# A Mamba, attention and mixture-of-experts layer pair on one core: wide state scans with the carried state in the tile, convolution made ahead, last attention in two halves

## The chip, the core and the metric

The kernel runs on one core of a Trainium2 chip. The core has TensorE (PE) for matrix products, VectorE (DVE), ScalarE (ACT) and GpSimd (POOL) for elementwise work, and SyncE (SP), which here only issues DMAs; 16 DMA engines move data between DRAM and the on-chip memory (SBUF), and matrix products land in a small accumulator memory (PSUM). The metric is the device time of one launch in microseconds, the median of several runs. All data are 32-bit floats.

## What is computed

The input is 8 images of 256 channels and 32 x 32 pixels, taken as 8 sequences of 1024 tokens with 256 features. Layer 0 is a Mamba block with a feed-forward block behind it, layer 1 attention with a mixture of experts behind it. Cut to what matters here:

```python
# layer 0, per image: x is [1024 tokens, 256]
xm, z = split(layernorm(x) @ W_in)                       # 512 features each
xm = silu(sum(shift(xm, k) * conv_w[:, k] for k in range(4)) + conv_b)
dt, Bm, Cm = split(xm @ W_x)                             # 16, 16 and 16 features
dt = softplus(dt @ W_dt + b_dt)
for t in tokens:                                         # 512 features x 16 states
    h = exp(dt[t] * A) * h + dt[t] * xm[t] * Bm[t]
    y[t] = sum_over_states(h * Cm[t])
x = x + ((y + xm * D) * silu(z)) @ W_out
x = x + gelu(layernorm(x) @ W1 + b1) @ W2 + b2
# layer 1
q, k, v = heads(layernorm(x))                            # 8 heads of 32
t = x + concat(softmax(q k' / sqrt(32) + column_bias) v) @ Wo + bo
u = layernorm(t)
w = softmax(mean_over_tokens(u) @ Wr + br)               # one routing per image, top 2 of 8 experts
out = t + layernorm(u + sum(w[e] * expert(e, u) for e in top2))
```

The recurrence over `t` is the heart of it: 512 x 16 independent first-order recurrences of 1024 tokens for each of 8 images.

## The kernel before

**Tiling.** Features lie on the 128 partitions, tokens along the free dimension. Each image is cut into two chunks of 512 tokens, so there are 16 chunks, 0 to 15; an even chunk is the first half of an image, an odd one the second. The 512 inner features are four groups of 128, handled as two halves of two groups. A chunk has 32 *steps*: 16 states times two halves. One step works on a tile of 128 partitions x 2 rows x 512 tokens (1024 elements).

**A step** (g = 0 to 511). `decay` (line 891) lets ScalarE make exp(dt * A) for both rows into `da_all`, which has two places, used in turn. `inputs` (908) lets VectorE multiply xm * dt by the row B of that state into a slot `hb` of the pool h4. `scan` (920) runs the recurrence in place on VectorE with the scan instruction. In an even chunk the state starts at zero, and one scan of 1024 elements covers both rows: `decay` keeps the first decay factor of the second row at zero, which restarts the recurrence there. In an odd chunk the state comes from the even one, each row has its own, and there are two scans of 512 elements with the tile `state` as their start value. After an even step, GpSimd copies the last column into `state`. `sums` (943) lets VectorE multiply by the row C, and GpSimd issues a DMA that adds the tile onto the accumulator `dx` of that half; the slot is free again when this DMA has landed. There are four such slots, and a fifth (the memory of the weight `w_z`) once all gates are made.

**Streams around the steps.** Everything else is written as Python generators ("streams"), and a small model of the queues' times (line 62) decides at build time where in each engine's instruction order their parts are put: after each part of a step `advance` (2129) emits what the model has as ready, more urgent kinds first (`URGENT`). The engines then run these orders as they were written, each in its own order; nothing is reordered on the chip. The streams are:

- `park` (958): for chunks 2 to 15, far ahead, layer norm, both halves of W_in, and storing the convolution's input (`xin_d`) and silu(z) (`sz_d`) in DRAM.
- `prologue(i)` (685): for chunks 2 to 15 it calls `conv_parked` (635), which loads the convolution's input with its shifts from DRAM, convolves it and applies Silu; then dt by softplus, whose terms GpSimd adds with accumulating DMAs, and the rows B and C. It starts at step FRONT[i-1] of the chunk before. CONV[i] chooses the convolution: four multiply-accumulate passes, the first on ScalarE and three on VectorE (0), or products with diagonal weights `taps` on TensorE (1). SOFT[i] chooses between two forms of softplus: 1 saves a VectorE operation for one more accumulating DMA.
- `gate_part` (991) loads silu(z) at step GATE[i]; `epilogue` (1039) follows after the chunk's last step: gating, W_out, layer norm, the feed-forward block.
- `attention` (1540): image by image, when the epilogues of both its chunks are done. It works through 32 units (two head groups x two query chunks x eight key blocks): scores on TensorE, Exp on ScalarE, products with v on TensorE; the denominators are products on TensorE too, but for the last image they are sums on VectorE (`dsum`).
- `route` (1717) and the experts: small VectorE operations choose two experts, GpSimd gathers their weights with six indirect DMAs per expert, and the products run on TensorE.

Where TensorE would sit idle, filler products ("warm") are put in, so that its clock stays up. Line 98 of the profile is the helper through which all compute instructions go, line 95 that of the DMAs.

Of the kernel before, what the change touches and what calls it, by code (L numbers as in the profile page):

```python
# [17 lines left out]
P = 128  # L18
B, C, L = 8, 256, 1024
KC = C // P  # L20
CH = 512
# [33 lines left out]
def hybrid_kernel(ctx: ExitStack, tc: tile.TileContext, a: dict, out: bass.AP):  # L55
# [46 lines left out]
    def vec_cost(op, out, *ins):  # L102
        n, into = width(out), str(out)
        chained = op == "scalar_tensor_tensor" and vec.into == into
        vec.into = into
        if op == "tensor_tensor_scan":
            return (0.125 if n == CH else 0.07) + n * 2.08e-3
        return (0.2 if n < P else 0.065) + n * 1.04e-3 + 0.2 * chained
# [42 lines left out]
    w_z = load("w_z", [P, KC, DI], a["W_in"].rearrange("(k p) n -> p k n", p=P)[:, :, DI:])  # L151
# [28 lines left out]
    mean_c = const.tile([P, 1], F32, name="mean_c")  # L180
    pool.memset(mean_c, 1.0 / C)
    mean_w = mean_c.to_broadcast([P, P])
    zero_c = const.tile([P, 1], F32, name="zero_c")
    pool.memset(zero_c, 0.0)
    zero_w = zero_c.to_broadcast([P, P])
    pick = const.tile([P, 4], F32, name="pick")
# [3 lines left out]
    wm_out = const.tile([P, ND], F32, name="wm_out")  # L190
    wm_2 = const.tile([P, HID // P], F32, name="wm_2")
    wm_o = const.tile([P, KC], F32, name="wm_o")
    mean_b = const.tile([P, 1], F32, name="mean_b")
    pick3 = const.tile([P, 4], F32, name="pick3")
    eps_t = const.tile([P, 1], F32, name="eps_t")
# [9 lines left out]
    bq4 = const.tile([P, NG], F32, name="bq4")  # L205
    bk4 = const.tile([P, NG], F32, name="bk4")
# [7 lines left out]
    bq4s = const.tile([P, NG], F32, name="bq4s")  # L214
    ok = const.tile([P, 1], F32, name="ok")
    qs = const.tile([P, 1], F32, name="qs")


    conv_tail = const.tile([P, NCH, ND, KW - 1], F32, name="conv_tail")

# [15 lines left out]
    bad = const.tile([P, 1], F32, name="bad")  # L236
    loads_e = const.tile([P, E], F32, name="loads_e")
    rev_e = const.tile([P, E], F32, name="rev_e")
    base1 = const.tile([P, KC], F32, name="base1")
    base2 = const.tile([P, NF], F32, name="base2")  # L240

    xin_d, t_d, xf_d, x1_d, xc_d, mu_d, mus_d = {}, {}, {}, {}, {}, {}, {}
# [29 lines left out]
    FRONT = (7, 13, 4, 4, 1, 14, 10, 1, 13, 1, 10, 6, 1, 5, 10)  # L272
    GATE = (20, 4, 30, 30, 22, 7, 30, 18, 28, 25, 5, 28, 30, 30, 12, 26)
    CONV = (0, 0, 0, 1, 1, 0, 0, 0, 0, 0, 0, 0, 0, 1, 0, 0)
    SOFT = (1, 0, 0, 1, 0, 0, 0, 0, 1, 0, 1, 0, 0, 0, 0, 0)

    POLL, PARK = -1.0, 2

# [37 lines left out]
    class Owner:  # L318


        def __init__(self, slots, peak, gives=0, held=0):
            self.slots, self.peak, self.gives, self.held = slots, peak, gives, held
            slots.owners.append(self)

        def take(self, name):
            while not (self.slots.ready() and self.slots.safe(self)):
                yield POLL
            self.held += 1
            return self.slots.now(name)
# [66 lines left out]
    def layernorm(  # L396
# [9 lines left out]
        if kept is not None:  # L406
# [10 lines left out]
            if kept < PARK:  # L417
                row = work_pool.tile([P, KW - 1 + CH], F32, name=f"row_{name}", tag="xp", bufs=2)
                row = row[:, :P]
# [13 lines left out]
            yield model.end if kept < PARK else max(landed, model.end)  # L433
            kept_at = sp.dma_start(xc_d[kept], dst)
# [120 lines left out]
    def conv_dve(i, xn, mem):  # L555
# [4 lines left out]
        for d in range(ND + 2):  # L560
            if d > 2 and d % 2:
                for t in range(1, KW):
                    for n in (d - 3, d - 2):
                        y = xm[n // 2][:, n % 2, :]
                        vec.scalar_tensor_tensor(
                            y, xps[n][:, t : t + CH], V("conv_w", n * KW + t), y,
                            ALU.mult, ALU.add,
                        )
            if 0 < d <= ND:
                h, q = divmod(d - 1, 2)  # L570
                xp = work_pool.tile([P, KW - 1 + CH], F32, name=f"xp_{i}_{d}", tag="xp", bufs=2)
                xps.append(xp)
                act.copy(xp[:, : KW - 1], conv_tail[:, c, d - 1, :])
                act.activation(xp[:, KW - 1 :], ps, AF.Identity, bias=b_in[:, d - 1 : d])
                banks.put(ps)
                if c < NCH - 1:
                    act.copy(conv_tail[:, c + 1, d - 1, :], xp[:, CH:])
# [16 lines left out]
    def conv_pe(i, xn, mem):  # L594
# [3 lines left out]
        while not set_up:  # L598
            yield POLL
        xm, xp, ps, ps2 = [], None, None, None  # L600
        for d in range(ND + 1):
            if d < ND:
                if d % 2 == 0:
                    xm.append((yield from mem.take(f"xm_{i}_{d // 2}")))

                ps2 = yield from banks.take(f"xin_{i}_{d}")
                for k in range(KC):
                    pe.matmul(
                        ps2, w_in[:, k, d * P : (d + 1) * P], xn[:, k, :],
                        start=(k == 0), stop=(k == KC - 1),  # L610
                    )
            if d:
                for t in range(KW):
                    for r in range(4):
                        rows = slice(HD * r, HD * r + HD)
                        pe.matmul(
                            ps[rows, :], taps[rows, (d - 1) * KW + t, :], xp[rows, t : t + CH],
                            start=(t == 0), stop=(t == KW - 1),
                        )
                if c < NCH - 1:  # L620
                    act.copy(conv_tail[:, c + 1, d - 1, :], xp[:, CH:])
            yield
            if d:
                h, q = divmod(d - 1, 2)
                act.activation(xm[h][:, q, :], ps, AF.Identity, bias=V("conv_b", d - 1))
                banks.put(ps)
            if d < ND:
                xp = work_pool.tile([P, KW - 1 + CH], F32, name=f"xp_{i}_{d}", tag="xp", bufs=2)
                act.activation(xp[:, KW - 1 :], ps2, AF.Identity, bias=b_in[:, d : d + 1])
                act.copy(xp[:, : KW - 1], conv_tail[:, c, d, :])  # L630
                ps = ps2
            yield
        return xm

    def conv_parked(i, mem):


        b, c = divmod(i, NCH)
        skip = 0 if c else KW - 1
        xm = []  # L640
        for h in range(NHALF):
            xps = []
            xm.append((yield from mem.take(f"xm_{i}_{h}")))
            for q in range(2):
                xp = work_pool.tile([P, KW - 1 + CH], F32, name=f"xp_{i}_{h}_{q}", tag="xp", bufs=2)
                landed = sp.dma_start(
                    xp[:, skip:], xin_d[b][h, :, q, c * CH - (KW - 1) + skip : (c + 1) * CH]
                )
                if skip:
                    act.copy(xp[:, :skip], conv_tail[:, 0, 0, :])  # L650
                xps.append(xp)
            yield landed
            if CONV[i]:
                for q in range(2):
                    d = 2 * h + q
                    ps = yield from banks.take(f"cv_{i}_{d}")
                    for t in range(KW):
                        for r in range(4):
                            rows = slice(HD * r, HD * r + HD)
                            pe.matmul(  # L660
                                ps[rows, :], taps[rows, d * KW + t, :], xps[q][rows, t : t + CH],
                                start=(t == 0), stop=(t == KW - 1),
                            )
                    yield
                    act.activation(xm[h][:, q, :], ps, AF.Identity, bias=V("conv_b", d))
                    banks.put(ps)
                continue
            for q in range(2):
                d = 2 * h + q
                act.activation(  # L670
                    xm[h][:, q, :], xps[q][:, :CH], AF.Identity, bias=V("conv_b", d),
# [3 lines left out]
            for t in range(1, KW):  # L675
                for q in range(2):
                    y = xm[h][:, q, :]
# [1867 lines left out]
```

## Time and profile before

| | us |
|---|---|
| median of three runs (3398.92 to 3409.55) | 3402.78 |
| the profiled execution | 3395.24 |
| its span, first to last instruction | 3393.4 |
| VectorE busy | 2993.7 |
| TensorE busy, fillers of the tile "warm" included | 3141.3 |
| fillers of the tile "warm" | 366.0 |
| ScalarE busy | 2467.8 |
| GpSimd busy | 1104.5 |
| HBM, mean over the span | 107 GB/s |

The profile is one execution on the chip. Its page gives each engine's busy time, the span cut in 40 slices with the busy share of each in tenths, the DMA queues, the chain that ended last, and groups of equal instructions: engine, operation, output tile <- input tiles, shape, count, then busy time and mean length of one in ns, then the idle time of the engine before them and what ended it. The trace behind it can be asked for stages, single instructions in order of time, and waits ("engine tile line <- what it waited for: total us, times, longest"). Buffer numbers are left out of the tiles' names, and a slot in the memory of `w_z` appears under that name.

### The profile page before, as it was taken

The numbers are of one execution on the slowest core, as the hardware profiler recorded it, in microseconds if no ns is written. First come the engines' busy times: TensorE is split into PE (matmuls) and PEld (weight loads), VectorE is DVE, ScalarE is ACT, GpSimd is POOL, SyncE is SP. The second block draws the span as 40 slices with busy tenths as digits, with TensorE's granted clock in tenths as the row PEclk, the third lists the DMA queues.
The fourth block names the chain that finished last, engine by engine and source line by source line (L and its number), as shares of the span: only waits on it lengthen the run. The fifth ranks groups of instructions, "written<-read, shape, count | busy, mean of one in ns | idle before, by whom it ended". The sixth has DMA issues, their size and how long they took to land. (4 is left out here: it accounts for less than half of the span.)

```text
span 3393.4 us, 44585 instructions
## 1 busy us (share of the span) xinstructions
PE 3141.3 (93%) x16359; PEld 1387.0 (41%) x16359; DVE 2993.7 (88%) x3140; ACT 2467.8 (73%) x3610; POOL 1104.5 (33%) x1072
## 2 busy tenths in 40 slices
PE   8888988999899999999999899999899989999998
PEld 5444443433343334333444344333443343334343
DVE  6999999899999979899999999999999999962561
ACT  4766756678867887687779777787768868864643
POOL 0242145313432235334353245133542453211010
PEclk9989989999999999999999999999999989999999
DMA  4877899989988898889998999799998998972140
GB/s 138 237 204 189 218 219 219 227 209 232 222 218 228 195 214 202 211 206 217 225 250 190 224 228 216 185 217 219 232 237 201 227 224 186 211 171 71 39 96 23
DMA packets 216134, 668.21 MB, mean 197 GB/s; under 512 B 31200, under 2 KB 42592, under 8 KB 215904
## 3 DMA queue, kind: packets, MB, share of 16 engines
q0 software_dynamic: 106112, 373.88, 56.5%
q1 hardware_dynamic: 109792, 291.38, 25.3%
q8 instruction: 130, 2.13, 0.2%
q14 instruction: 100, 0.82, 0.1%
HBM read 269.20 MB, written 92.93 MB: 107 GB/s over the span
## 5 line engine op out<-in xcount | busy, mean ns | idle before, releaser
L98 ACT ACTIVATE da_all<-dt,vecs 128x512 f32<-128x512 f32 (+1 forms) x1024 | 699.4, 717 | 287.9 <-DVE hb L98 244.8
L95 POOL DMA_DIRECT2D dx<-hb x449 | 397.3, 890 | 1363.5 <-DVE hb L98 960.8
L98 DVE TENSOR_TENSOR hb<-xm,bc 128x1024 f32<-128x1024 f32 x449 | 540.0, 1203 | 22.5 <-issue 19.8
L98 DVE TENSOR_TENSOR_SCAN hb<-da_all,state,hb 128x512 f32<-128x512 f32 x448 | 552.7, 1268 | 4.2 <-ACT da_all L98 4.1
L98 ACT ACTIVATE pt<-sc 128x1024 f32<-128x1024 f32 x512 | 494.6, 1018 | 81.5 <-PE sc L98 70.9
L98 DVE TENSOR_TENSOR hb<-hb,bc 128x1022 f32<-128x1022 f32 (+1 forms) x449 | 546.7, 1218 | 0.0
L98 DVE TENSOR_TENSOR_SCAN hb<-da_all,hb 128x1024 f32<-128x1024 f32 x225 | 514.2, 2285 | 8.3 <-ACT da_all L98 8.3
L98 PE MATMUL warm<-mean_c,zero_c 128*128 128x256 f32 x1182 | 366.0, 433 | 48.9 <-ACT z L98 11.5
L98 POOL COPY state<-hb 128x2 f32<-128x2 f32 x225 | 330.6, 1471 | 206.4 <-DVE hb L98 201.2
L98 PE MATMUL sc<-qk,qk 32*128 32x512 f32 x2048 | 337.7, 647 | 18.2 <-ACT pt L98 17.1
L98 PEld LDWEIGHTS warm<-mean_c,zero_c 128*128 128x128 f32 x1182 | 219.6, 206 | 191.7 <-PE warm L98 73.3
L98 PE MATMUL num<-pt,v 128*32 128x512 f32 x2048 | 279.6, 616 | 13.2 <-DVE ot L98 13.2
L98 PE MATMUL den<-pt,ecb 128*32 128x512 f32 x1792 | 239.0, 604 | 0.0
L98 PE MATMUL re<-he,g 128*128 128x512 f32 x472 | 221.6, 615 | 18.5 <-ACT sz L98 7.8
L98 PE MATMUL facc<-fh,w 128*128 128x512 f32 x512 | 232.8, 601 | 5.9 <-ACT fo L98 2.4
L98 PE MATMUL fh<-x_f,w 128*128 128x512 f32 x480 | 227.1, 604 | 7.2 <-DVE x_f L98 2.5
L98 PE MATMUL he<-xe,g 128*128 128x512 f32 x448 | 219.0, 615 | 5.7 <-issue 3.5
L98 ACT ACT_TABLE_LOAD x159 | 204.0, 1283 | 3.5 <-PEq L2532 0.7
L98 PEld LDWEIGHTS sc<-qk,qk 32*128 32x128 f32 x2048 | 101.0, 185 | 198.3 <-ACT pt L98 80.3
L98 PEld LDWEIGHTS facc<-fh,w 128*128 128x128 f32 x512 | 95.4, 192 | 132.3 <-issue 118.1
L98 PEld LDWEIGHTS re<-he,g 128*128 128x128 f32 x472 | 89.9, 196 | 133.2 <-issue 103.8
L98 PEld LDWEIGHTS fh<-x_f,w 128*128 128x128 f32 x480 | 86.5, 190 | 133.9 <-issue 100.3
(422 smaller groups left out, 4705.4 us busy)
## 6 DMA issues: line engine op xcount, KB each, us to landing
dx<-hb POOLq DMA_DIRECT2D x449, 512.0 KB, 7.8
bc<-bc_d SPq DMA_DIRECT2D x256, 512.0 KB
dx<-w_z POOLq DMA_DIRECT2D x63, 512.0 KB, 6.7
dt<-e POOLq DMA_DIRECT2D x36, 512.0 KB, 9.5
dt<-u POOLq DMA_DIRECT2D x30, 512.0 KB, 11.4
xin_d<-z SPq DMA_DIRECT2D x28, 512.0 KB
sz_d<-z SPq DMA_DIRECT2D x28, 512.0 KB
sz<-sz_d SPq DMA_DIRECT2D x28, 512.0 KB
```

Source lines behind the costliest of these rows:

```text
L95: f(*args, **kw)
L98: return f(*args, **kw)
```

## The change

**Two-row slots and wide scans.** The tiles of h4 and `da_all` get one more column per row, 2 x 513. Column 0 of each row of `da_all` is set to zero once. Column 0 of each row of `hb` holds the start value: zero in even chunks (set by GpSimd where the slot isn't clean), in odd chunks a copy of `state` that GpSimd makes in `inputs`. One scan of 1026 elements then serves both kinds of chunk. The accumulator `dx` becomes 2 x 513 as well, and the accumulating DMA moves 1025 elements from the second column on.

```diff
     def inputs(g):
+        if i % NCH:
+            pool.at = max(pool.at, vec.at)
+            pool.tensor_copy(hb[:, :, 0], state[:, s, 2 * h : 2 * h + 2])
+            das[g, 2] = pool.at + 0.3
+            clean.discard(id(hb))
+        elif id(hb) not in clean:
+            pool.at = max(pool.at, vec.at)
+            pool.memset(hb[:, :, 0], 0.0)
+            das[g, 2] = pool.at + 0.3
+            clean.add(id(hb))
-        vec.tensor_tensor(hb, xd, bc[:, 0, :].unsqueeze(1).to_broadcast([P, 2, CH]), ALU.mult)
+        vec.tensor_tensor(
+            hb[:, :, 1:], xd, bc[:, 0, :].unsqueeze(1).to_broadcast([P, 2, CH]), ALU.mult
+        )
-    def scan(g, q):
+    def scan(g):
...
-        if c == 0:
-            if q:
-                both = hb.rearrange("p a t -> p (a t)")
-                vec.tensor_tensor_scan(
-                    both, da_all[:, g % 2].rearrange("p a t -> p (a t)"), both, 0.0,
-                    ALU.mult, ALU.add,
-                )
-        else:
-            vec.tensor_tensor_scan(
-                hb[:, q, :], da_all[:, g % 2, q, :], hb[:, q, :], state[:, s, d : d + 1],
-                ALU.mult, ALU.add,
-            )
+        for q in range(3):
+            vec.at = max(vec.at, das.pop((g, q), 0.0))
+        vec.tensor_tensor_scan(
+            flat(hb), flat(da_all[:, g % 2]), flat(hb), 0.0, ALU.mult, ALU.add
+        )
     def sums(g):
-        me["landed", h] = pool.dma_start(out=me["acc", h], in_=hb, accum_op=ALU.add)
+        me["landed", h] = pool.dma_start(
+            out=me["acc", h][:, 1:], in_=flat(hb)[:, 1:], accum_op=ALU.add
+        )
```

In the loop over steps the two decays of step g+2 now both follow the one scan of step g.

**Convolution and Silu ahead.** `park` now convolves and applies Silu for chunks 2 to 15 and stores the result (`xm_d`) in place of the convolution's input; `prologue` loads it. `conv` replaces `conv_pe` and `conv_parked`. The tables change; in CONV, chunks 2 to 6, 8 and 9 are on TensorE (3, 4 and 13 before), in SOFT chunk 1 alone (3, 8 and 10 before; entry 0 is used by neither).

```diff
     def prologue(i: int):
-        mem = Owner(t4, 8, 6)
+        mem = Owner(t4, 9, 6)
         if i < PARK:
...
         else:
-            xm = yield from conv_parked(i, mem)
-        for t in xm:
-            act.activation(t, t, AF.Silu)
-        lnexp()
+            xm = []
+            for h in range(NHALF):
+                xm.append((yield from mem.take(f"xm_{i}_{h}")))
+                landed = sp.dma_start(xm[h], xm_d[i][h])
+            yield landed
     def park():
-            xi = yield from gates(i, mem, xn, 0)
+            xm = yield from (conv if i else conv_first)(i, xn, mem)
+            for t in xm:
+                act.activation(t, t, AF.Silu)
+            lnexp()
             yield
             for h in range(NHALF):
-                mem.put(xi[h], at=sp.dma_start(xin_d[b][h, :, :, c * CH : (c + 1) * CH], xi[h]))
+                mem.put(xm[h], at=sp.dma_start(xm_d[i][h], xm[h]))
-    FRONT = (7, 13, 4, 4, 1, 14, 10, 1, 13, 1, 10, 6, 1, 5, 10)
-    GATE = (20, 4, 30, 30, 22, 7, 30, 18, 28, 25, 5, 28, 30, 30, 12, 26)
-    CONV = (0, 0, 0, 1, 1, 0, 0, 0, 0, 0, 0, 0, 0, 1, 0, 0)
-    SOFT = (1, 0, 0, 1, 0, 0, 0, 0, 1, 0, 1, 0, 0, 0, 0, 0)
+    FRONT = (4, 13, 2, 8, 2, 7, 11, 18, 14, 8, 1, 4, 7, 5, 19)
+    GATE = (27, 7, 13, 30, 30, 18, 29, 15, 23, 21, 6, 26, 27, 30, 24, 27)
+    CONV = (1, 0, 1, 1, 1, 1, 1, 0, 1, 1, 0, 0, 0, 0, 0, 0)
+    SOFT = (1, 1, 0, 0, 0, 0, 0, 0, 0, 0, 0, 0, 0, 0, 0, 0)
```

The start of the diagonal weights `taps` is moved ahead of the other one-time work, the model's VectorE costs are refined, and a rule (`spare`) keeps some of the 25 large SBUF slots free for the prologue before `park`, the experts and the attention take theirs.

**Last attention in halves.** `attention_last` handles the eighth image. It starts when the epilogue of chunk 14 is done and the attention before it has ended, makes q, k and v of that chunk, and runs the 8 units whose queries and keys both lie in it; after the epilogue of chunk 15 it does the other 24. Both head groups keep a sum open in PSUM.

```diff
+        yield from operands(0)
...
+        yield from run_units([(g, 0, j) for g in range(NG) for j in range(NT // 2)])
+        while ("e", b * NCH + 1) not in done:
+            yield POLL
...
+        yield from operands(1)
+        yield from run_units(
+            [(g, 0, j) for g in range(NG) for j in range(NT // 2, NT)]
+            + [(g, 1, j) for g in range(NG) for j in range(NT)]
+        )
```

**Joined routing.** In `route` the row numbers for both weight matrices, and both bias vectors of an expert, are made by one operation each where there were two: seven small VectorE operations per image for fourteen.

## The prediction

> **What bounds the kernel now.** I read the page first, then busy time by stage, then VectorE's waits, then the order of single instructions.
>
> ```profile
> span 3393.4 us, 44585 instructions
> PE 3141.3 (93%) x16359; PEld 1387.0 (41%) x16359; DVE 2993.7 (88%) x3140; ACT 2467.8 (73%) x3610; POOL 1104.5 (33%) x1072
> DVE  6999999899999979899999999999999999962561
> DMA  4877899989988898889998999799998998972140
> ```
>
> VectorE (DVE) is full until slice 35 and nearly idle after it: a scan stage, then a tail. The last scan step ends at 3014 us. By stage (us, then busy time of PE, PEld, DVE, ACT, POOL, then granted clock, DMA share, GB/s):
>
> ```profile
> 64.00:3014.00 2950.00, 2737.99 (x14374) 1194.65 (x14375) 2815.40 (x2793) 2252.69 (x3320) 1064.42 (x1017) 0.96 0.90 215
> 3014.00:3093.00 79.00, 76.15 (x460) 36.23 (x455) 20.83 (x61) 34.93 (x54) 14.10 (x15) 1.00 0.46 111
> 3093.00:3126.00 33.00, 33.00 (x100) 17.52 (x99) 2.45 (x2) 13.94 (x18) 2.31 (x3) 1.00 0.19 63
> 3126.00:3270.00 144.00, 142.83 (x800) 51.97 (x800) 93.58 (x149) 99.91 (x116) 9.15 (x9) 1.00 0.28 59
> 3270.00:3394.00 124.00, 103.02 (x382) 54.74 (x377) 25.68 (x73) 35.07 (x52) 12.85 (x13) 0.95 0.13 40
> ```
>
> In the scan stage VectorE is busy 2815 of 2950 us and idle 135; TensorE's 2738 hold 307 of its filler matmuls (the tile "warm"), so 2431 are work. The tail is the last epilogue (79), the operands of the last attention (33), its 32 units beside the seventh image's experts (144), and the last experts (124). VectorE's waits in the scan stage:
>
> ```profile
> DVE hb L98 <- issue: 19.8, 5, 5.2
> DVE hb L98 <- ACT da_all L98: 12.4, 11, 3.0
> DVE hb L98 <- DMA dx<-hb: 2.5, 3, 1.6
> ```
>
> The scans wait for almost nothing. POOL never holds a scan up today, since nothing a scan reads is written by it.
>
> **The change, part by part.** The sums are made against the profiled execution, 3395.2 us (span 3393.4 and 1.8 around it); the median of the runs shown, 3402.8, is 7.6 higher, and I carry differences over to it.
>
> *Wide scans.* First an odd chunk's step, then an even one's:
>
> ```profile
> 1844.99 2.45 DVE L98 TENSOR_TENSOR_SCAN hb<-da_all,state,hb 128x512 f32<-128x512 f32 x2
> 1847.36 1.19 DVE L98 TENSOR_TENSOR hb<-xm,bc 128x1024 f32<-128x1024 f32 x1
> ...
> 1645.88 2.29 DVE L98 TENSOR_TENSOR_SCAN hb<-da_all,hb 128x1024 f32<-128x1024 f32 x1
> 1648.09 1.20 DVE L98 TENSOR_TENSOR hb<-xm,bc 128x1024 f32<-128x1024 f32 x1
> ```
>
> From a scan's start to the next instruction, two narrow scans take 2.37 us, a wide one 2.21: 0.16 over 256 odd steps, 41. Two more elements per step (2 ns each, from 2.21 against a narrow 1.19) cost 512 x 0.004 = 2. **-39.** The decays of an odd step can no longer start after the first half scan; even steps live with that at 9 us of waits in all (8.3 and 1.0), so nothing to +5: counted 0.
>
> *The carried state.* An odd step's state now comes by a POOL copy into the tile's first column ("copy-in"), which the scan waits for. Behind that scan on VectorE are the next inputs and sums, behind them the next accumulating DMA on POOL and the decays on ScalarE: a late copy delays the whole step. POOL works in order, and the copy for step g+2 stands behind the accumulating DMA of step g:
>
> ```profile
> 2523.59 2.45 DVE L98 TENSOR_TENSOR_SCAN hb<-da_all,state,hb 128x512 f32<-128x512 f32 x2
> 2532.19 2.45 DVE L98 TENSOR_TENSOR_SCAN hb<-da_all,state,hb 128x512 f32<-128x512 f32 x2
> ...
> 2527.10 5.99 POOL L95 DMA_INDIRECT g<-eW_d,rows  x1 [0.30 <-issue]
> 2537.10 1.03 POOL L95 DMA_DIRECT2D dx<-w_z  x1
> ```
>
> The sums of step g end as the first scan starts, its DMA goes out 14 us later behind a burst of six expert gathers, and the scan two steps on starts 6 us before that DMA's end. Today nobody waits; after the change that scan does. Over the 240 such pairs of odd steps I took the time from the end of POOL's issue to the start of the scan two steps on. In 37 it is under 1.5 us; the shortfalls add up to 85 us taken singly, 48 if one delay of VectorE also covers those right behind it (35 for a need of 0.5 us). Even steps, where POOL already makes a copy per step, show the queue with that load: 75 covered, 189 singly. I take 40, nearest to the odd row: **+40**, ends 30 and 75, and 189 as the outer end.
>
> A rule of the Trainium skill bears on the price of a copy. The row: state copies take 181 ns at best, 1031 in the median and 5502 at most, and those that start within one VectorE instruction end some 0.1 us into a later one. "SBUF — State Buffer", section "SBUF: two separate sides", says that VectorE with two SBUF inputs and a GpSimd operation that reads SBUF lock each other out for a whole instruction. By the rule a copy could also hold VectorE up: 256 x 0.18 = 46, so the wide scans would gain nothing. By the row it doesn't: a wide scan has its 2.2 us to the next start with a copy in its wake as without. I take the row, 0, and leave 46 to the range.
>
> *The accumulating DMA* moves 1025 elements from 4 bytes into the row, 4100 B for 4096. "DMA: Bandwidth & Descriptors", section "How a descriptor splits into AXI transactions", has a transfer that starts off a 256 B boundary pay for an added transaction: 129 beats for 128 (an estimate from the page), 1%. The nearest row, the 2060 B packets of the convolution's loads, which start off the boundary in DRAM, took 101 ns against 92 for 2048 B: 10%. The 4096 B packets of POOL's queue take 332 ns, eight per engine and DMA, 512 DMAs: 1360 us, so 14 or 136 us of each engine in a stage where the DMA share is 0.90. Landings (7.8 us in the median) are due after two steps (9 us); I take the page's 1% and count 0; the row's end is a rival.
>
> *Convolution ahead.* The same accumulations move from each prologue into the stream that prepares chunks early; chunks on TensorE go from 3 to 7, so VectorE does 9 instead of 13:
>
> ```profile
> L98 DVE SCALAR_TENSOR_TENSOR xm<-xp,vecs,xm 128x512 f32<-128x512 f32 x156 | 105.4, 741 | 7.8 <-ACT xm L98 7.8
> ```
>
> That is 12 per chunk at 0.67 us (105.4/156): 48 fewer, **-32**. TensorE gains four times 14.2 us (the tile "cv": 42.7 for three chunks), 57, under the fillers, of which 139 us lie before 490 us, where those chunks are prepared; without that cover it would be +57 on TensorE. Stores stay at two 512 KB on SP's queue per chunk, loads go from four of 257 KB to two of 512 KB: bytes equal, two issues fewer. Silu and its table loads move with it at equal count. Some 56 more tail copies at 0.19 us on ScalarE (11 us) lie in its 700 idle us.
>
> *SOFT* falls from three chunks to one: four more VectorE instructions of 1.23 us, **+5**, and four accumulating DMAs fewer. *Joined routing* halves 18.8 us of small operations (rows 3.0, t 5.9, hbias 3.0, obias 2.7 and 4.2); six of eight images are routed before the scans end: **-7**. The retimed starts (FRONT, GATE) act on the 135 idle us: 0, with 25 either way.
>
> *Last attention in halves.* Its first 8 of 32 units and half its operands need only chunk 14. The seventh attention's last exponential is at 3025, so they start after it, beside the last epilogue. TensorE's work between 3014 and 3270 is 252 less fillers (8.7, 0.6, 24.3): 218 of 256, so at most 37 can go; 8 units at 144/32 = 4.5 also give 36. The epilogue shares TensorE with them, so I take two thirds, **-25**, ends 0 and -37. If the seventh attention ends later against the scans, all of it goes.
>
> Sum: -39 + 40 - 32 + 5 - 7 - 25 = **-58**: 3337 in the profiled execution, **3345** for the median.
>
> **Rivals.** (B) POOL is in time: waits of 10 and the tail's full 37: -39 + 10 - 32 + 5 - 7 - 37 = -100, 3303. For it: copies are short and the bursts rare. Against: every image has two bursts. (C) **Slower: the copy-in sets the pace of odd chunks.** POOL's queue with a copy and a DMA per step drains as slowly as in even chunks, and each shortfall counts singly: 189, with 10 of tail gain left: -39 + 189 - 32 + 5 - 7 - 10 = +106, 3509; half of that, 95, gives +12. It decides from waits of about 83, or 0.32 us per odd step. (D) The scans end earlier but TensorE's backlog takes it back: from 2490 on it is busy 502 of 524 us with only 20 of fillers. Only half of the scan stage's -33 and 10 of the tail stay: -26, 3377. (E) Off-boundary packets cost 10%: DMA share 0.90 to 0.95, landings miss their two steps; POOL then blocks on landings; if two thirds of the 136 turn up as waits, +90 on the sum: 3435.
>
> **How the numbers follow.** Chances: forecast 0.48 (own range 3310 to 3385), B 0.17, C 0.16, D 0.13, E 0.06. A change under 0.3%, 10 us, can't be told from none here. Faster: 0.46 of the forecast, B, 0.11 of D: 0.74. Same: 0.02 of each of the forecast, D and C: 0.06. Slower: 0.14 of C, E: 0.20. The range leaves out the upper half of C and the ends below B less the 25 of retiming: 3275 to 3430.
>
> **What the profile will show.** Odd steps with one scan of 1026 elements and 2.2 us to the next start; VectorE waits of the kind "hb for POOL hb", 30 to 75 us in all, mostly beside gathers; 108 convolution accumulations, all before about 1300 us; scan stage 33 shorter; the first 8 units before the last epilogue's end. Wrong if those waits pass 83, if the tile "dx" lands later than two steps, or if the tail keeps its 379 us.

## The result and the profile after

The changed kernel takes 3395.5 us (median, 3382.5 to 3404.2) against 3403.0 for the kernel before on the same chips: ratio 0.9972, 95% interval 0.9961 to 0.9983. That is 7.5 us faster, where 58 had been forecast. The interval leaves out 1, but the gain stays under the 0.3% that the forecast had named as the least to be told from none. The profiled execution took 3400.7 us, 5 more than the median.

VectorE did get its relief. First the page, then busy time by stage with the columns of the stage table of before (start, scans, last epilogue, second operands, units, last experts):

```profile
span 3398.9 us, 44984 instructions
PE 3154.1 (93%) x16661; PEld 1357.4 (40%) x16661; DVE 2921.4 (86%) x2784; ACT 2454.0 (72%) x3646; POOL 1254.8 (37%) x1361
DVE  5989999989999999997999999899989998963541
DMA  3777999789999999888998999989998997873140
```

```profile
0.00:79.00 79.00, 62.69 (x349) 37.59 (x350) 42.20 (x77) 31.13 (x50) 2.14 (x19) 0.94 0.41 121
79.00:3018.00 2939.00, 2737.66 (x14605) 1163.28 (x14604) 2736.97 (x2436) 2231.00 (x3344) 1211.26 (x1300) 0.96 0.90 215
3018.00:3115.00 97.00, 97.00 (x511) 41.91 (x514) 36.74 (x82) 56.18 (x78) 13.90 (x14) 1.00 0.41 87
3115.00:3128.00 13.00, 13.00 (x127) 6.15 (x124) 5.09 (x8) 5.98 (x10) 0.45 (x1) 1.00 0.10 42
3128.00:3262.00 134.00, 133.89 (x672) 51.43 (x670) 72.59 (x113) 88.87 (x103) 9.30 (x10) 1.00 0.20 52
3262.00:3399.00 137.00, 109.83 (x408) 56.99 (x404) 27.76 (x70) 40.88 (x62) 17.77 (x18) 0.92 0.27 66
```

VectorE's busy time falls from 2993.7 to 2921.4, and in the scan stage from 2815 to 2737. The stage itself only falls from 2950 to 2939. VectorE's idle time in it rises from 135 to 202 us. The table counts from the first step's inputs to the last step's sums:

| | before | after |
|---|---|---|
| first step at | 64.3 | 78.6 |
| scan stage | 2950.2 | 2939.2 |
| VectorE busy in it | 2815.6 | 2737.4 |
| VectorE idle in it | 134.6 | 201.8 |
| from the last sums to the end | 378.9 | 381.1 |

What VectorE waited for in the scan stage:

```profile
DVE h L98 <- POOL h L98: 38.8, 14, 7.5
DVE h L98 <- ACT da_all L98: 20.1, 13, 3.9
DVE xm L98 <- ACT dx L98: 12.3, 3, 10.7
DVE e L98 <- ACT u L98: 12.1, 5, 4.1
DVE x_f L98 <- PE var_f L98: 10.3, 5, 2.8
DVE yl L98 <- POOL state L98: 9.2, 2, 4.8
DVE tn_t L98 <- PE var_t L98: 9.0, 5, 4.0
DVE sq_a L98 <- PE var_a L98: 8.4, 6, 2.5
```

The first row is the new wait for the copy-in. With 1.6 us on the fifth slot it makes 40.4. The second, for decays, was 12.4 before. The other rows are short waits for single links of norms, gates and softplus. One late copy, from the order of single instructions on POOL and on VectorE:

```profile
1526.46 1.38 POOL L95 DMA_INDIRECT g<-in_eW,r  x1 [0.31 <-ACT pt L98]
...
1533.97 0.95 POOL L95 DMA_INDIRECT g<-eW_d,r  x1 [0.30 <-DMA dx<-h]
1534.91 0.20 POOL L98 COPY h<-state 128x2 f32<-128x2 f32 x1
```

```profile
1529.13 1.22 DVE L98 TENSOR_TENSOR h<-h,bc 128x1024 f32<-128x1024 f32 x1
1535.15 2.30 DVE L98 TENSOR_TENSOR_SCAN h<-da_all,h 128x1026 f32<-128x1026 f32 x1 [4.80 <-POOL h L98]
1537.36 1.20 DVE L98 SCALAR_TENSOR_TENSOR e<-u,e 128x1024 f32<-128x1024 f32 x1
```

The copy takes 0.20 us, but stands behind six expert gathers. The scan waits 4.8 us for it. From a wide scan's start to the next instruction there are 2.2 us, as forecast.

### The profile page after: what moved, and what is told of

Same layout as the page of the kernel before. It is cut to its first block, busy times and chain, and to the rows that moved or that the text cites. A ratio compares the mean times of both kernels' runs of the same rounds, so it can differ in the third digit from the quotient of the medians.

```text
span 3398.9 us, 44984 instructions
## 1 busy us (share of the span) xinstructions
PE 3154.1 (93%) x16661; PEld 1357.4 (40%) x16661; DVE 2921.4 (86%) x2784; ACT 2454.0 (72%) x3646; POOL 1254.8 (37%) x1361
## 5 line engine op out<-in xcount | busy, mean ns | idle before, releaser
L98 DVE TENSOR_TENSOR_SCAN h<-da_all,h 128x1026 f32<-128x1026 f32 x468 | 1070.6, 2288 | 60.6 <-POOL h L98 38.8
L98 ACT ACTIVATE da_all<-dt,vecs 128x512 f32<-128x512 f32 x1024 | 680.6, 716 | 312.8 <-DVE h L98 286.0
L95 POOL DMA_DIRECT2D dx<-h x468 | 414.5, 886 | 1262.7 <-DVE h L98 653.7
L98 DVE TENSOR_TENSOR h<-xm,bc 128x1024 f32<-128x1024 f32 x468 | 563.6, 1204 | 13.3 <-DMA dx<-h 7.1
L98 DVE TENSOR_TENSOR h<-h,bc 128x1024 f32<-128x1024 f32 (+1 forms) x468 | 569.5, 1217 | 0.0
L98 POOL COPY state<-h 128x2 f32<-128x2 f32 x237 | 300.4, 1281 | 243.3 <-DVE h L98 233.3
L98 PE MATMUL warm<-small 128*128 128x256 f32 x898 | 285.1, 437 | 49.2 <-ACT dt L98 10.9
L98 POOL COPY h<-state 128x2 f32<-128x2 f32 x231 | 273.7, 1185 | 0.0
L98 PE MATMUL num<-pt,v 128*32 128x512 f32 x1792 | 245.1, 620 | 9.9 <-DVE ot L98 9.9
L98 PEld LDWEIGHTS warm<-small 128*128 128x128 f32 x898 | 165.6, 206 | 175.9 <-PE warm L98 62.6
```

The lines of the kernel that those rows point to most:

```text
L95: f(*args, **kw)
L98: return f(*args, **kw)
```

## The experiments

The changed kernel's ratio, 0.9972, is what each is held against. 0.1 points of a ratio are 3.4 us. In the first three and in the reliefs the written order of the instructions is the changed kernel's: the planner's costs are booked as before, only the instruction is missing or another.

### The copy-in and the wide scans

Copy-in left out:

```diff
-            pool.tensor_copy(hb[:, :, 0], state[:, s, 2 * h : 2 * h + 2])
+            model.do(pool, pool_cost("tensor_copy"))
```

> Against the changed kernel (3395.5 us): POOL's copy of the carried state into the first column of a step's tile is left out in the odd chunks, so these scans start from a wrong state; the order of all other instructions is the same. Theory W (the copy-in is paid in full: VectorE's 39 us of waits for POOL were all on the path): 3357, ratio to the kernel before 0.986 to 0.988, VectorE's idle time in the scan stage 202 to about 163. Rival H (the order of the other engines is what VectorE waits for; the waits for POOL hide other waits, which appear in their place): at most half of it, 3376 to 3395, ratio 0.992 to 0.998, with more waits for ScalarE's da_all or for TensorE.

3377.9 us, 0.9896 (0.9864 to 0.9927), 18 below the changed kernel by the medians, 26 by the ratios. The scan stage is 19 shorter, at 2920.3. Half of the 39 us comes back as other waits, between the two theories:

```profile
DVE h L98 <- ACT da_all L98: 22.6, 13, 4.0
DVE e L98 <- ACT u L98: 18.4, 5, 7.4
DVE h L98 <- DMA dx<-h: 14.8, 7, 8.0
```

The waits for `u` were 12.1 and those for `dx` 7.1 with the copies in. The scans themselves take 2288 ns on average with and without copies beside them.

Wide scans undone in odd chunks:

```diff
-        vec.tensor_tensor_scan(flat(hb), flat(da_all[:, g % 2]), flat(hb), 0.0, ...)
+            for q in range(2):
+                nc.vector.tensor_tensor_scan(
+                    hb[:, q, 1:], da_all[:, g % 2, q, 1:], hb[:, q, 1:],
+                    state[:, s, 2 * h + q : 2 * h + q + 1], ALU.mult, ALU.add)
```

> The changed kernel with the wide scans of odd chunks undone: two scans of 512 per step that take the carried state as their first value, and no copy-in; the order of all else is the same. Theory W (wide scans save 39 us of VectorE and their copy-in costs 39): VectorE 39 busier, waits for POOL gone, time 3395 within 8, ratio 0.995 to 1.000. Rival H (the waits for POOL hid others): slower than the changed kernel by 20 to 35, ratio 1.003 to 1.008. Rival D (the decays of an odd step start late behind one wide scan, and cost more than is seen): faster by 10 or more, ratio under 0.994.

3390.7 us, 0.9936 (0.9903 to 0.9969). VectorE is 39 busier (2776.5) and its idle time 45 less (157.1). So both terms of the forecast, -39 and +40, are measured as VectorE's time, and together the wide scans and their copy-in gain nothing: undoing them is 5 us faster by the medians (theory W), 12 by the ratios (rival D), with intervals that overlap. The waits for decays, 12 us here and 20 in the changed kernel, speak for D. Against the first run, 41 us more VectorE work cost only 13 us, though with decays that come in time more often (12 us of waits against 23).

Copy-in on VectorE, at the same place:

```diff
-            pool.tensor_copy(hb[:, :, 0], state[:, s, 2 * h : 2 * h + 2])
+            model.do(pool, pool_cost("tensor_copy"))
+            nc.vector.tensor_copy(hb[:, :, 0], state[:, s, 2 * h : 2 * h + 2])
```

> The changed kernel with the copy-in on VectorE in place of POOL, at the same place in the order. Theory W: 231 copies of two columns at 0.07 to 0.12 us are 16 to 28 us of VectorE, the 39 us of waits for POOL go: 3372 to 3385, ratio 0.991 to 0.995. Rival H (those waits hid others): the 16 to 28 are added and less than 20 is gained: 3390 to 3405, ratio 0.996 to 1.001.

3387.7 us, 0.992 (0.9887 to 0.9952), 8 below the changed kernel by the medians and 18 by the ratios. Theory W holds by the ratio. A copy shows as 149 ns, more than expected, 38 us in all; but it overlaps the instructions around it, and VectorE is only 16 us busier in the stage. This is the lowest median here of a kernel that computes everything, below both kernels compared; the run before it lies within the noise of it.

### The start

```diff
-                xp = yield from xp2.take(f"xp_{i}_{d}")
+                xp = xp2.now(f"xp_{i}_{d}")
```

> The changed kernel with chunk 0's convolution taking its two row buffers at once, as the kernel before does, in place of waiting in the order for the planner's time at which they are free. Theory S (the 15 us by which the first scan starts later, 79 for 64, are added to the end): first scan at 62 to 68, time 3378 to 3385, ratio 0.993 to 0.995; the planner's order of the rest moves with it, which can add or take some 15. Rival: the start is caught up later (VectorE would wait elsewhere for the same transfers and set-up), time within 5 of 3395.

The first step moves from 78.6 to 68.6, and nothing comes of it: 3400.6 us, 0.9977 (0.9957 to 0.9998). Chunk 2 begins at 477 us, in the changed kernel at 473, in the kernel before at 481. The late start, which the forecast had overlooked, is caught up within two chunks (the order of the rest moved with this edit).

### The tail

```diff
-            while ("e", (B - 1) * NCH) not in done:
+            while ("e", B * NCH - 1) not in done:
```

> The changed kernel with the last attention's two halves both started only once the last chunk's epilogue is done, as in the kernel before. Theory F (TensorE is full from the scans' end to the last unit, 240 us of work in 244, so an early start cannot shorten it and only puts off the last epilogue and the seventh image's experts): time within 8 of 3395, ratio 0.995 to 1.000. Theory of the forecast (the early start is worth 25): 3413 to 3425, ratio 1.003 to 1.006. Rival G (halves cost, since the seventh image's last expert is pushed into the last image's gathers): 3380 to 3388, ratio 0.993 to 0.995.

3412.9 us, 1.0026 (1.0007 to 1.0045): the early start is worth 17 us (tail 396.5 against 381.1), nearer to the forecast's 25 than to theory F's nothing. Its stages, with the changed kernel's columns (to the second operands, to the last unit, last experts):

```profile
3016.00:3120.00 104.00, 101.86 (x540) 48.94 (x540) 22.59 (x57) 47.71 (x73) 19.30 (x20) 1.00 0.42 96
3120.00:3284.00 164.00, 163.53 (x850) 62.38 (x850) 94.81 (x150) 109.86 (x128) 8.93 (x9) 1.00 0.24 56
3284.00:3412.00 128.00, 105.95 (x380) 55.32 (x378) 24.72 (x66) 35.05 (x52) 12.73 (x13) 0.93 0.17 45
```

But then the tail without halves has grown from 378.9 to 396.5. After the scans' end TensorE spends 93 us on products of the experts (`he` and `re`) in this run, 94 in the changed kernel and 80 in the one before: in the changed kernel the last products of the sixth image's experts run at 3036 to 3048, behind the scans' end, where they had run at 2993 to 3003, ahead of it. And the halves have a price behind the units: the last experts take 137 us, here 128, in the kernel before 124. The seventh image's results are then still moving while the last image's gathers start (first gathers 6.5 us to landing against 3.6 before).

### Relief, one engine at a time

Each of these leaves work out and keeps the order. VectorE's part of the convolution, and then TensorE's:

```diff
-                    vec.scalar_tensor_tensor(y[:, q, :], xps[q][:, t : t + CH], ...)
+                    model.do(vec, vec_cost("scalar_tensor_tensor", ...))
```

> The changed kernel with VectorE's share of the convolution ahead left out (three of four taps of the chunks that TensorE doesn't do, chunk 0 excepted): 96 instructions of 0.67 us, 64 us of VectorE, in the same order as all else. Theory F (VectorE sets the pace of the scan stage, one for one, as the forecast counted it): 3332, ratio 0.976 to 0.981. Theory M (VectorE arrives earlier at waits that the fixed order keeps; the wide and narrow scans without copy-in stood 41 us of VectorE apart and 13 of time, a third): 3365 to 3382, ratio 0.988 to 0.994, VectorE's idle time in the scan stage up by 40 or more.

```diff
+                            if t:
+                                model.do(pe, pe_cost("matmul", ...))
+                                continue
```

> The changed kernel with three of the four taps of every convolution on TensorE left out (the order of all else is the same): some 75 us less TensorE work (seven chunks of 14.2, three quarters), all before 1800 us. Theory P (TensorE is the second bound: in chunks 6 to 8, with 181, 196 and 172 us of work of its own, it sets the pace, and what VectorE was relieved of is lost there): chunks 3 to 8 together 25 to 50 us shorter, time 3345 to 3370, ratio 0.983 to 0.990. Theory V (VectorE and the order of its waits set the pace; TensorE has its fillers to give): under 10 us, time 3386 to 3396, ratio 0.994 to 0.998.

The second with the copy-in left out as well:

> Both edits of the first and fifth experiment: without the copy-in (the carried state is left out in odd chunks) and with one tap of four on TensorE. Theory P (copy-in waits and TensorE hide each other, so that removing one alone shows half): more than the sum of the two alone, 40 or more below the changed kernel plus what the fifth gives. Theory V (the two have nothing to do with each other): 18 below the fifth.

ScalarE's decays shortened, and the accumulating DMAs:

```diff
+        nc.scalar.activation(da[:, :400], chunk[i]["dt"][h][:, q, :400], AF.Exp, ...)
```

> The changed kernel with decays of 400 of each 512 columns (the rest stays at zero): 1024 decays of 0.07 us less, some 70 us of ScalarE, the order of all else the same. Theory F (ScalarE's 700 idle us cover it): time within 6 of 3395, ratio 0.995 to 0.999. Theory A (VectorE's waits for decays and for other ScalarE results, some 60 us by the chain of waits, are ScalarE being late): 3360 to 3380, ratio 0.987 to 0.993.

```diff
+        nc.gpsimd.dma_start(out=dst[:, :769], in_=flat(hb)[:, 1:770], accum_op=ALU.add)
```

> The changed kernel with the last quarter of every accumulating DMA left out (3076 for 4100 B per partition), so some 340 us less of each of the 16 DMA engines' 2645 in the scan stage, the order of all else the same. Theory F (transfers are hidden): time within 8 of 3395, ratio 0.995 to 1.000. Theory Q (a DMA share of 0.90 holds loads and landings up, and VectorE's short waits everywhere come of it): 30 or more faster, 3340 to 3370, ratio under 0.990, landings of dx from 7.1 us to under 6.

All of them together, and TensorE's experts:

> All the reliefs at once, in the order of the changed kernel: no copy-in (the carried state is left out in odd chunks), VectorE's 96 convolution taps left out, one tap of four on TensorE, decays of 400 columns of 512, three quarters of each accumulating DMA. Taken singly their ratios stand 0.76, 0.32, 0.08, 0.42 and 0.60 points below the changed kernel's 0.9972, 2.2 together. Theory M1 (waits in a fixed order that hide each other: what one engine is relieved of waits for another): more than the sum, ratio 0.945 to 0.970. Theory M2 (each has stretches of its own where it decides): the sum, 0.972 to 0.980, 3307 to 3335.

```diff
+                            if i:                  # products with g1
+                                model.do(pe, pe_cost("matmul", ps, w))
+                                continue
...
+                            if f % 2:              # products with g2
+                                model.do(pe, pe_cost("matmul", ps, w))
+                                continue
```

> The changed kernel with half of the matrix products of the experts of images 1 to 7 left out (every second term of both products; order of all else the same): 16 of 0.617 and 16 of 0.608 us per image, 20 us of TensorE each, some 117 in chunks 5 to 15, where TensorE has few fillers, and 20 in the tail. The fifth experiment's relief lay in chunks 0 to 4 alone (all convolution accumulations on TensorE are there), so it said nothing of the later ones. Theory P (TensorE decides where its own work nearly fills a chunk: 181, 197 and 172 us in chunks 6 to 8, of 199, 213 and 188): scan stage shorter by 40 to 100, chunks 6 to 8 by 8 or more each, tail by 10 to 20; 3280 to 3345, ratio under 0.983. Theory W (VectorE's waits come of the written order, not of one engine's work): scan stage shorter by 15 or less, tail by 10 to 20; 3362 to 3385, ratio 0.987 to 0.994.

| relief | taken away in the scan stage, us | scan stage shorter, us | median, us | ratio (95%) |
|---|---|---|---|---|
| VectorE: taps | 61 | 10 | 3387.5 | 0.9940 (0.9915 to 0.9966) |
| TensorE: taps, chunks 0 to 4 | 59 | -1 | 3392.1 | 0.9964 (0.9949 to 0.9978) |
| the same without copy-in | 59 and the copies | 10 | 3382.3 | 0.9934 (0.9910 to 0.9957) |
| ScalarE: decays | 92 | 16 | 3380.5 | 0.9930 (0.9906 to 0.9953) |
| DMA: accumulation | 298 of each engine | 25 | 3374.1 | 0.9912 (0.9887 to 0.9938) |
| TensorE: experts | 100 | 10 | 3358.9 | 0.9879 (0.9852 to 0.9906) |
| all above but the experts, copy-in left out | | 51 | 3342.8 | 0.9811 (0.9775 to 0.9848) |

(298 is the difference of the accumulating queue's packet times in the stage, 1850 us of each engine, 62.9% of the stage, against 1552.) The stages of the first row and of the last, with the columns of the stage table:

```profile
78.00:3007.00 2929.00, 2729.35 (x14607) 1161.39 (x14605) 2676.52 (x2341) 2230.33 (x3344) 1183.18 (x1300) 0.96 0.91 216
79.00:2967.00 2888.00, 2666.47 (x13936) 1146.64 (x13935) 2671.32 (x2340) 2136.48 (x3344) 991.14 (x1044) 0.96 0.82 196
```

A stage is read from one execution, and the changed kernel's twenty executions lie 22 us apart, so a single stage figure is rough. The ratios, from all executions, say 11 us for VectorE's taps, 14 for the decays, 20 for the accumulation and 55 for all together. By either reading no engine's work in the scan stage is worth more than a fifth of what is taken away. That VectorE counts one for one (F of its run) falls. P falls too as far as tested, both where TensorE has fillers and, in the run with fewer products of the experts, where it has few.

But in these two runs the granted clock was lower in every execution, 0.952 to 0.957 and 0.944 to 0.947, against 0.960 to 0.967 for the changed kernel, and TensorE's other products were slower (those of the tile `sc` took 656 and 667 ns in the mean, 651 before). The 59 and 100 us are net of that; what TensorE's work is worth at an unchanged clock isn't shown.

ScalarE's run ends at the edge of its theory A, the DMA engines' between F and Q; both are worth more than nothing. Without the copy-in the TensorE run gains 10 us more, less than either of its theories said. Taken singly the reliefs in the joint run, with 19 for the copy-in, add up to 69 us of the stage; together they give 51. So no second engine masks the first (M1 falls), and the sum isn't quite reached either, though the joint run's interval runs into the range of M2. What VectorE does with the 61 us, in the run without its taps:

```profile
DVE h L98 <- ACT da_all L98: 43.1, 20, 9.5
DVE h L98 <- POOL h L98: 39.2, 14, 7.5
DVE xe L98 <- PE mu_a L98: 13.3, 4, 9.9
```

It comes earlier to the same scans and waits for decays 43 us instead of 20; its idle time in the stage rises by 51.

The tail is another matter. Scan stage and tail of the run with fewer products of the experts:

```profile
77.00:3006.00 2929.00, 2639.91 (x14237) 1109.29 (x14237) 2736.74 (x2437) 2225.72 (x3344) 1213.04 (x1300) 0.94 0.90 216
3006.00:3356.00 350.00, 322.27 (x1633) 141.85 (x1632) 141.63 (x273) 190.87 (x252) 41.40 (x42) 0.98 0.30 72
```

With 27.5 us of fillers in either tail, TensorE's own work in it goes from 326 to 295 us, 31 less, and the tail from 381 to 350: one for one.

### Other orders

Here the written order changes. The table CONV of the kernel before (three chunks on TensorE):

```diff
-    CONV = (1, 0, 1, 1, 1, 1, 1, 0, 1, 1, 0, 0, 0, 0, 0, 0)
+    CONV = (0, 0, 0, 1, 1, 0, 0, 0, 0, 0, 0, 0, 0, 1, 0, 0)
```

> The changed kernel with the convolution on TensorE for three chunks, as in the kernel before, and VectorE doing the other four: 48 more accumulations at 0.67 us, 32 us, TensorE 57 less; the planner's order moves with it, which can add or take some 15. Theory V (VectorE sets the pace): 3415 to 3435, ratio 1.003 to 1.009. Theory P (TensorE takes back what VectorE is relieved of): 3385 to 3402, ratio 0.994 to 0.999.

3468.9 us, 1.0195 (1.0164 to 1.0226), 73 slower than the changed kernel. VectorE is 31 busier in the scan stage and 32 idler, so less than half is its added work; both theories fall.

The taps of VectorE left out as above, but with the planner counting nothing for them, and the copy-in on VectorE with the planner told:

```diff
-                    vec.scalar_tensor_tensor(y[:, q, :], xps[q][:, t : t + CH], ...)
+                    pass
```

> As the ninth experiment (96 convolution taps of VectorE left out, 64 us), but the planner counts them at nothing too, so the order of all engines follows. Theory O (it is the order planned for a busier VectorE that keeps the waits): faster than the ninth by 20 or more, 3340 to 3367, ratio under 0.989. Theory C (the waits belong to the data, or the timetable was fitted to this load and suits no other): not faster than the ninth, 3380 to 3415, ratio 0.993 to 1.003.

```diff
-            pool.tensor_copy(hb[:, :, 0], state[:, s, 2 * h : 2 * h + 2])
-            das[g, 2] = pool.at + 0.3
+            vec.tensor_copy(hb[:, :, 0], state[:, s, 2 * h : 2 * h + 2])
```

> The copy-in on VectorE as in the third experiment, but with the planner told (0.2 us on VectorE each, no wait for POOL): the order of all engines follows. Theory O: as fast as the third or faster, 3370 to 3388, ratio up to 0.992. Theory C: 3390 to 3420, ratio 0.996 to 1.005.

3440.1 us, 1.0103 (1.0064 to 1.0142), and 3432.0 us, 1.0077 (1.0057 to 1.0098). The same work in the changed kernel's order took 3387.5 and 3387.7. So a planner that knows of the new load makes, with these start steps, an order that is 44 to 53 us worse, and theory C holds, beyond its own ranges.

```diff
-    FRONT = (4, 13, 2, 8, 2, 7, 11, 18, 14, 8, 1, 4, 7, 5, 19)
+    FRONT = (4, 13, 2, 8, 2, 7, 11, 14, 14, 8, 1, 4, 7, 5, 19)
```

> The copy-in on VectorE as in the third experiment, and the prologue of chunk 8 started at step 14 of chunk 7 in place of 18. In chunk 7 VectorE waits 10.7 us for that prologue's dx before the next chunk's inputs. If that wait is the chunk's loss: 10 below the third, 3375 to 3380, ratio 0.988 to 0.991. If the earlier start only takes other work's turn: 3385 to 3400, ratio 0.992 to 0.999.

3445.7 us, 1.012 (1.0081 to 1.0158): one start step moved by four is 58 slower than the third run, whose copy-in it has. Chunks 8 and 9 take 206 and 199 us, in the third run 190 and 179.

Then the start steps of the kernel before, in the changed kernel (all of FRONT and GATE):

```diff
-    FRONT = (4, 13, 2, 8, 2, 7, 11, 18, 14, 8, 1, 4, 7, 5, 19)
+    FRONT = (7, 13, 4, 4, 1, 14, 10, 1, 13, 1, 10, 6, 1, 5, 10)
```

> The changed kernel with the 31 start steps (FRONT and GATE) of the kernel before, all else as changed. Theory O (the order is fitted to one load of the engines, and another one leaves VectorE waiting at prologues' ends): 3430 to 3480, ratio 1.008 to 1.023, VectorE's busy time as in the changed kernel and its idle time 40 or more higher. Theory of the forecast (new starts act only on idle time, 25 either way): 3370 to 3420, ratio 0.990 to 1.004.

3494.4 us, 1.028 (1.0256 to 1.0303): 99 slower. VectorE's work in the scan stage is the same (2733.8), its idle time 271 instead of 202, and the tail 405. Chunk 5 alone, its columns as above, and what VectorE waited for in it:

```profile
996.00:1245.00 249.00, 239.84 (x1265) 88.91 (x1264) 173.75 (x146) 186.64 (x257) 70.66 (x81) 0.95 0.69 166
```

```profile
DVE e L98 <- ACT u L98: 31.0, 2, 19.3
DVE h L98 <- POOL h L98: 22.6, 2, 17.7
```

It takes 249 us where the changed kernel takes 174. TensorE is busy for 240 of them: this timetable piles up in one chunk what the new one spreads, and single waits reach 19 us.

Last, one such step moved in the kernel before:

```diff
-    FRONT = (7, 13, 4, 4, 1, 14, 10, 1, 13, 1, 10, 6, 1, 5, 10)
+    FRONT = (7, 13, 4, 4, 1, 14, 10, 5, 13, 1, 10, 6, 1, 5, 10)
```

> The kernel before with one of its 31 start steps moved: the prologue of chunk 8 begins at step 5 of chunk 7 in place of 1. Theory O: this order was fitted as well, so one number costs 20 to 60: 3420 to 3460, ratio 1.006 to 1.018. Rival (only the changed kernel's order is brittle): within 12 of 3403, ratio 0.996 to 1.004.

3406.5 us, 1.0021 (1.0009 to 1.0034), 8 slower than the kernel before beside it, so the rival holds as far as one step can tell. It is the start of the same chunk, moved by as many steps, that cost 58 us in the changed kernel's order.

## Why the prediction was wrong

**The step that failed** is the sum's premise, that VectorE's time in the scan stage is the kernel's time: "VectorE (DVE) is full until slice 35", "The scans wait for almost nothing", and then each saved VectorE microsecond counted as one of time. The sizes were right: -73 of VectorE forecast, -72 measured; waits for the copy-in 40 forecast, 40.4 measured. But 61 us of VectorE work, taken away in a fixed order, gave 10 of scan stage, and 41 put back cost 13. At that rate, a sixth to a third, the 78 us of relief in the scan stage would be worth 13 to 26 (an estimate), and the 40 us of new waits, of which half counts, cost 19. The stage, with its new timetable, gave 11. A busy share of 95% (2815 of 2950) said that VectorE is nearly always at work, not that the others could have kept up with a faster one. After the change TensorE, with its fillers, is busy for as long as VectorE (2738 and 2737 of 2939), and the DMA share is 0.90. That these stand close behind, in an order written for one pace, fits all runs, but no run names the link that holds.

**Retimed starts, "0, with 25 either way"**: the bound was four times too narrow. Old start steps cost the changed kernel 99 us, and four other edits that changed its order left it 36 to 73 slower; the one in the tail cost 17, and only the one at the start stayed within 5. VectorE's idle time in the scan stage rose by 67 us, and nearly half of that is in chunk 7 (before, then after, columns of the stage table):

```profile
1410.00:1581.00 171.00, 160.59 (x797) 58.47 (x796) 169.33 (x163) 140.11 (x191) 46.67 (x49) 0.98 0.90 207
1375.00:1588.00 213.00, 202.44 (x1016) 84.10 (x1016) 179.72 (x178) 168.52 (x239) 76.98 (x87) 0.98 0.83 206
```

VectorE is idle there for 2 us before and 33 after, while TensorE is busy for 202 of the 213. With the old start steps chunk 7 takes 179 us, and chunk 5 the 249 shown above: the start steps decide which chunk gets the pile. How the edits would look with tables fitted to each of them was not tried, nor the new start steps in the kernel before, so what the moved convolution would be worth with its best timetable stays open; by the three-chunk run, -32 for four chunks on TensorE is VectorE's part of 73.

**Wide scans and the carried state** netted +1 in the forecast; by the run that undid both they cost 5 to 12 us, not clear of the noise. The later decays, counted 0, show as 7 to 8 us more of waits. By the Trainium skill ("SBUF — State Buffer", section "SBUF: two separate sides") the copies could have held VectorE up; 2288 ns per scan of an odd chunk with them and without agree with the row that was taken, 0.

**The accumulating DMA**: hardly slower packets, as chosen. In the trace the 4100 B packets take 339 ns in the mean, the queue's 4096 B packets before took 333, so 2% where 1% and 10% had been weighed. The queue's share of the stage is 62.9% (before 62.8%), landings 7.1 us (before 7.8). Rival E falls. The transfers are not free for all that: a quarter of them is worth 25 us of the stage.

**Last attention in halves**: -25 forecast, 17 measured against a late start of both halves. The cap of 37 was wrong, though: the fillers between 3126 and 3270 are 5.9 us, and the 24.3 that I subtracted is about what lies in the stage behind it (24.55). TensorE's own work was 237 of 256, and from the scans' end to the last unit at most 19 could go; that stretch fell from 256 to 244. Why the tail got no shorter: without halves it would have grown by 18, of which the sixth image's experts behind the scans' end are 13 and the last experts 4, and the halves took back 15. Why those experts slipped behind the scans was not tested.

**Not in the sum**: the first step starts 14 us later. Taking 10 of them back gained nothing.

**Joined routing and SOFT** (-7, +5) were not tried singly; the measured sum of VectorE's work has both.

**Rivals**: none came in as written. D, TensorE's backlog, has the nearest size (3377) and is right for the tail, where TensorE decides one for one; in the scan stage 100 us of its work gave 10. C is refuted by its own mark, waits of 40 against 83. One of the named signs of being wrong came true: the tail kept its 379 us (381). Of the other signs, the first half's units before the last epilogue's end came true (from 3065 us; that epilogue's products end at 3115), the scan stage 33 shorter didn't (11), and the 108 convolution accumulations last until 1800 us, not 1300.

**What stays open**: which links hold the scan stage. Chunk 7 takes 208 to 217 us in all runs that keep the order, whatever was relieved; with 13 us less of TensorE's products in it it takes 209. The start step meant to take out the largest single wait in it (10.7 us for `dx` before a chunk's inputs) lost more elsewhere. No run left out the fillers, 227 us of the stage, which stand in TensorE's order like any other product.

## What to carry to other kernels

When several engines follow one written order, find the exchange rate before counting a relief: leave the work out with the order kept, and see how much of it the clock gives back (here 61 us for 10; in the tail, with one engine full, 31 for 31). A change that brings new start steps with it is two changes; here the old steps would have cost more (99 us) than the whole forecast gain (58), and a bound of 25 on them was a guess that no row supported. For a filler or wait that is subtracted from a stage, read it from that stage's own row.

## What the runs showed of the hardware

A two-column copy shows as 149 ns on VectorE, but 256 of them made VectorE only 16 us busier. On POOL it took 200 ns in the row above, where VectorE stood idle, and the state copies of the same size, most of them beside a busy VectorE, have a mean of 1281 ns; the scans do not get longer by it (2288 ns). The 4100 B packets that start 4 bytes into the row took 339 ns, 4096 B ones before 333. Where half of the experts' products were left out, the clock granted to the remaining ones was lower (0.94 in the scan stage of that run, 0.96 in the changed kernel).
